# The opening of a two-layer image kernel: first image kept on chip, layer 1's parameters loaded singly, its first rows, queries and values earlier

## The chip, the core and the metric

The kernel runs on one core of a Trainium2 chip. The core has a matrix engine (TensorE, PE in the profile; loading a weight tile into it is listed as PEld), three engines for element-wise work (VectorE or DVE, ScalarE or ACT, GpSimd or POOL) and a sync engine (SP), which here does nothing but issue transfers. Each engine takes its instructions in order and waits at an instruction until its inputs are there and its output buffer is free. Tiles lie in an on-chip memory of 128 partitions, SBUF; matmuls write to a smaller one, PSUM; arrays that fit in neither lie in device memory and are moved by DMA. SP and ACT each have a DMA queue of their own. The metric is the device time of one execution in microseconds (us), as the median of several.

## What is computed

Everything is float32. The input is eight images of 256 channels and 64 x 64 pixels. Two residual layers follow one another, each behind a normalisation over groups of 8 channels of a whole image.

```python
x = x + _L0_conv_ref(_gn(x), ...)
x = x + _L1_conv_ref(_gn(x), ...)

# layer 0
x1 = _conv1x1(x, w1, b1)                  # 32 channels
x2 = _conv1x1(x, w2, b2)                  # 32 channels
x3 = _conv1x1(x, w3, b3)                  # 256 channels
h = relu(_bn(concatenate([x1, _unfold3(reflect_pad(x2))])))
h = relu(_bn(_conv1x1(h, cw1)))           # 32 channels
w = _conv1x1(h, cw2, cb2).reshape(B, G, K * K, H, W)     # 32 groups, 9 taps
x3u = _unfold3(zero_pad(x3)).reshape(B, G, SHARE, K * K, H, W)
out = einsum('bgskhw,bgkhw->bgshw', x3u, w)

# layer 1
q, k, v = three 1x1 convolutions, 256 to 256 channels, 4 heads
att = softmax(q . (unfold7(k) + unfold7(position)))      # 49 neighbours
out_att = sum over the neighbours of att * unfold7(v)
wts = softmax over 9 of einsum('oc,bchw->bohw', Wfc, x)  # 9 weights per channel
oc = nine depthwise pairs: _dwconv(relu(_dwconv(x, w1)), w2)
out_conv = sum over 9 of oc * wts
return rate1 * out_att + rate2 * out_conv
```

So a band of pixels of layer 0 needs the rows of x3 above and below it, and layer 1 of an image needs the statistics of all of layer 0's output for that image.

## The kernel before

**Tiling.** Each image is cut into NB = 8 bands of R = 8 rows (512 pixels); the 256 channels are NCT = 2 tiles of 128. A tile of one band and all channels is 512 KB. All 64 bands of layer 1 are done one after the other by a main loop over g; layer 0 runs AHEAD = 12 bands in front, so the loop starts at g = -12, and for g below 0 only layer 0 is at work ("alone" in the code).

**Order.** The order of the instructions on each engine is the order of the code (`manual_schedule`, L963). Each g has STEPS = 8 steps s, and each step calls `advance()` six times. `after(n, f)` (L215) puts f behind n further advances; that is how work is staggered by hand. For each step `steer(g, s)` (L941) issues loads and statistics, and `beside(g, s)` (L869) gives two lists of work: `mid` runs in the middle of the step, `end` at its end.

**One band of layer 0**, spread over several g:

- `load_x` (L97) brings 512 KB of x into a tile. `first_stats` (L275) calls it for the statistics of layer 0's normalisation and puts the statistics (L283, on DVE) n advances later. For the first image the eight bands go, in this order, into two tiles "xc", two "xr", one "xs" and three "yp" (L965 on). Only the two in "xc" are kept for the convolutions; `steer` loads the bands from 2 on a second time into "xc" at s = 0 of each g below 0 (L99 in the queue's timeline).
- At g, for band g + 12: `small_maps` (L320) computes x1 and x2 on PE, `write_maps` copies them out (L343 and L347 on ACT, edge copies on POOL), `value_maps` (L362) computes x3 (L369), copies it on ACT into x3n (L374) and stores it to device memory from SP.
- For band g + 11: `hidden_maps` (L409) does the first two steps towards the tap weights. `x_by_group` (L399) loads the residual x into "xg", and `values_by_group` (L381) reads x3 back with its neighbouring rows as "x3q" (L389 to L397). Both are laid out with the 32 groups times four pieces of a band on the partitions.
- For band g + 10: `tap_weights` (L441), once for each of three rows of taps. PE makes the weights of three taps (pw, L447); DVE makes the product of weights and x3q for each tap (L460), two product buffers "prod" in turn; POOL adds the product to xg (L468, six to nine of them a band). While layer 0 is alone, every third product goes instead into a "yp" tile and is summed by PE with an identity matrix (`gather`, L481), and DVE adds that sum to xg (`combine`, L488). Then come the statistics of layer 1's normalisation (L496) and the store of the new x as "x1" (L500, four DMAs from SP).

**Layer 1's parameters** are wq, wk, wv (256 KB each), wfc (eight of the nine weights, 2 MB), a mask for the scores, c2 (layer 0's last weights) and last, the ninth of Wfc. `load` at first only keeps their transfers in the list `late`. `layer1_loads` (L186) issues all of them on ACT's queue in one go, after the statistics of the first image. Three operations on them follow later on DVE: wv is scaled by rate1 (L195), and `last` is subtracted from each half of wfc (L200, 128 x 2048 elements):

```python
        for n, f in enumerate(layer1_loads()):
            after(4 * STEPS * (3 + n), f)
```

**Layer 1 begins** at g = 0. Before it, at g = -1, `beside` asks for the first image's first rows: `load_rows` (L528) reads band 0 into "yp" at s = 0 and band 1 at s = 1, from x1; `normalise` (L540, L543 on ACT) follows one and two steps later, a channel tile each. `values` (L551, PE L563, copies on ACT L572, L581) and `value_tile` (L601, PE L607, copy L609 into one of nine "vt" buffers) prepare the values; `position` (L616) makes the positional term on POOL; `queries` (L627, PE L637, ACT L641) and `keys` (L646, PE L658, DVE L666 and L673) prepare the first channel tile. Where the position, queries and keys go is set by these lines:

```python
        early = inx in (0, NB - 1)
        if 0 <= g + 1 < B * NB:
            if s == 5 - early:
                mid.append(lambda: position(bn, inx))
            if s == 6 - early:
                mid.append(lambda: queries(bn, inx, 0))
            if s == 7 - early:
                mid.append(lambda: keys(bn, inx, 0))
```

At g = -1 that is s = 4, 5 and 6; values come at s = 4 and 5, value tiles at s = 6 and 7, and the tap weights of band 9 at s = 0, 2 and 4. From g = 0 on, each step does one head pair of scores (`scores`, PE L703; DVE L712, which adds the mask and finds the maximum, is its first reader), `exponentials` (L720), `probabilities` (DVE L727, ACT L729), the transposition (L735) and the weighted sum (L747) of earlier steps, two of the eight `branch_weights` (PE L825, ACT L830) of a channel tile with the sums of them on POOL (L1026), and a share of the depthwise convolutions (DVE L782, L808).

Of the kernel before, what the change touches and what calls it, by code (L numbers as in the profile page):

```python
# [18 lines left out]
P = 128  # L19
C = 256  # L20
# [40 lines left out]
AHEAD = NB + 4  # L61
AHEAD0 = AHEAD + NB + 1
STEPS = NCT * NT // 2


TAPS_AT = (1, 3, 5), (0, 2, 4)
# [20 lines left out]
def conv_layers_kernel(ctx: ExitStack, tc: tile.TileContext, ins: dict, out: bass.AP):  # L87
# [5 lines left out]
    def x_tile(use, b, i):  # L93
        bufs = {"xs": 1, "xc": 2, "xr": 2}[use]
        return w0.tile([P, NCT, BAND], F32, tag=use, name=f"{use}_{b}_{i}", bufs=bufs)

    def load_x(b, i, use, t=None):  # L97
        t = x_tile(use, b, i) if t is None else t
        nc.sync.dma_start(  # L99
            out=t, in_=x_in[b].rearrange("(t p) n -> p t n", p=P)[:, :, i * BAND : (i + 1) * BAND]  # L100
        )
        return t


    late = []
# [1 line left out]
    def load(name, shape, src=None, now=True):  # L107
        t = const.tile(shape, F32, name=f"c_{name}")
        late.append(lambda: nc.scalar.dma_start(out=t, in_=ins[name] if src is None else src))
        if now:  # L110
            late.pop()()
        return t
# [12 lines left out]
    wk = load("wk", [P, NCT, C], ins["wk"].rearrange("(t p) n -> p t n", p=P), now=False)  # L125
    wv = load("wv", [P, NCT, C], ins["wv"].rearrange("(t p) n -> p t n", p=P), now=False)
    wfc_in = ins["wfc"].rearrange("(t p) k n -> p t k n", p=P)
    wfc = load("wfc", [P, NCT, KK - 1, C], wfc_in[:, :, : KK - 1], now=False)

    ident = const.tile([P, P], F32, name="ident")  # L130
    make_identity(nc, ident)
# [53 lines left out]

    def layer1_loads():  # L186


        last = w1.tile([P, NCT, 1, C], F32, tag="rec", name="last", bufs=1)
        for f in late:  # L190
            f()
        nc.scalar.dma_start(out=last, in_=wfc_in[:, :, KK - 1 :])

        def first():
            nc.vector.tensor_scalar(wv, wv, rate1, None, ALU.mult)  # L195

        def difference(kt):
            nc.vector.tensor_sub(wfc[:, kt], wfc[:, kt], last[:, kt].to_broadcast([P, KK - 1, C]))  # L200

        return [first, lambda: difference(0), lambda: difference(1)]

    class Image:
        def __init__(self):
# [66 lines left out]
        after(3, a1)  # L272


    def first_stats(b, i, use="xs", t=None, n=9):  # L275
        im = images[b]
        if i == 0:
            im.st0 = stat.tile([P, NCT, NB, 6], F32, tag="st", name=f"st0_{b}")
        x = load_x(b, i, use, t)

        def take():
            for ct in range(NCT):
                nc.vector.bn_stats(im.st0[:, ct, i, :], x[:, ct, :])  # L283

        after(n, take)
        return x
# [33 lines left out]
    def small_maps(b, i):  # L320


        im = images[b]

        p12 = ps.tile([P, R // 2, W], F32, tag="gen", name=f"p12_{b}_{i}", bufs=5)
        for kt in range(NCT):
            for u in range(2):
                nc.tensor.matmul(
                    p12[64 * u : 64 * u + 64], im.w12s[:, kt, :],
                    im.xc[i][:, kt, u * BAND // 2 : (u + 1) * BAND // 2],  # L330
                    start=(kt == 0), stop=(kt == NCT - 1),
                )
        return lambda: write_maps(b, i, p12)
# [28 lines left out]
    def value_maps(b, i, mt):  # L362

        im = images[b]
        if mt == 0:
            im.x3[i] = dram.tile([C, R, HP], F32, tag="x3", name=f"x3_{b}_{i}")
        p3 = ps.tile([P, BAND], F32, tag="gen", name=f"p3_{b}_{i}_{mt}", bufs=5)
        for kt in range(NCT):
            nc.tensor.matmul(  # L369
                p3, im.w3s[:, kt, mt * P : (mt + 1) * P], im.xc[i][:, kt, :],  # L370
                start=(kt == 0), stop=(kt == NCT - 1),
            )
        p3 = p3.rearrange("p (r c) -> p r c", r=R)
        nc.scalar.activation(x3n[mt][:, :, 1 : 1 + W], p3, AF.Identity, bias=im.bias[:, 1 + mt : 2 + mt])  # L374
        nc.sync.dma_start(out=im.x3[i][mt * P : (mt + 1) * P], in_=x3n[mt])
# [225 lines left out]
    def value_tile(b, j, u):  # L601
        im = images[b]
        n = min(R, WP - j * R) * KW
        pvt = ps.tile([CHUNK, 2, C], F32, tag="gen", name=f"pvt_{b}_{j}_{u}", bufs=5)
        for g in range(2):
            for ct in range(NCT):
                nc.tensor.transpose(pvt[:n, g, ct * P : (ct + 1) * P], im.vc[j, ct][:, 2 * u + g, :n], ident)  # L607
        vt = im.vt[j, u] = w1.tile([CHUNK, 2, C], F32, tag="vt", name=f"vt_{b}_{j}_{u}", bufs=9)
        nc.scalar.copy(vt[:n], pvt[:n])  # L609

    def new_keys(i):
# [257 lines left out]
    def beside(g, s):  # L869

        b, i = divmod(g, NB)
        bn, inx = divmod(g + 1, NB)
        mid, end = [], []

        early = i in (0, NB - 1)
        if g >= 0:
            if s == 2 - early:
                mid.append(lambda: queries(b, i, 1))
            if s == 3 - early:
                mid.append(lambda: keys(b, i, 1))  # L880
        early = inx in (0, NB - 1)
        if 0 <= g + 1 < B * NB:
            if s == 5 - early:
                mid.append(lambda: position(bn, inx))
            if s == 6 - early:
                mid.append(lambda: queries(bn, inx, 0))
            if s == 7 - early:
                mid.append(lambda: keys(bn, inx, 0))

        if g >= 0 and i < NB - 1:  # L890
            if s in (4, 5):
                mid.append(lambda: values(b, i + 2, s - 4))
            if s in (6, 7):
                end.append(lambda: value_tile(b, i + 2, s - 6))
        if g > 0 and i and s in (0, 1):
            mid.append(lambda: value_tile(b, i + 1, s + 2))
        if i == NB - 1 and 0 <= b + 1 < B:
            if s in (4, 5):
                mid.append(lambda: values(b + 1, 0, s - 4))
            if s in (6, 7):  # L900
                end.append(lambda: value_tile(b + 1, 0, 2 * s - 12))
                end.append(lambda: value_tile(b + 1, 0, 2 * s - 11))
        if g >= 0 and i == 0:
            if s == 0:
                mid += [lambda: values(b, 1, 0), lambda: values(b, 1, 1)]
                end.append(lambda: value_tile(b, 1, 0))
            if s in (1, 2):
                mid.append(lambda: value_tile(b, 1, 2 * s - 1))
            if s == 1:
                end.append(lambda: value_tile(b, 1, 2))  # L910

        nxt = [(b, i + 2, 0)] if g >= 0 and i + 2 < NB else []
        if i == NB - 1 and 0 <= b + 1 < B:
            nxt = [(b + 1, 0, 0), (b + 1, 1, 1)]
        for bb, ii, d in nxt:
            if s == d:
                end.append(lambda bb=bb, ii=ii: load_rows(bb, ii))
            if s in (d + 1, d + 2):
                end.append(lambda bb=bb, ii=ii, d=d: normalise(bb, ii, s - d - 1))

        alone = g < 0
        if 0 <= g + AHEAD < B * NB:
            bq_, iq = divmod(g + AHEAD, NB)
            if alone and s == 0:
                mid.append(lambda: small_maps(bq_, iq)())
            if s == (2 if alone else 0):
                (mid if alone else end).append(lambda: value_maps(bq_, iq, 0))
            if s == (3 if alone else 1):
                mid.append(lambda: value_maps(bq_, iq, 1))
        if 0 <= g + AHEAD - 1 < B * NB and s == (2 if alone else 1):  # L930
            at = (3, 7, 8, 12, 16) if alone else (5, 13, 14, 19, 21)
            end.append(lambda: hidden_maps(*divmod(g + AHEAD - 1, NB), at))
        if 0 <= g + AHEAD - 2 < B * NB and s in TAPS_AT[alone]:
            u = TAPS_AT[alone].index(s)
            end.append(
                lambda: tap_weights(*divmod(g + AHEAD - 2, NB), u, g < -1, PRODUCTS_AT[g < -1][u])
            )
        return mid, end

    def steer(g, s):  # L940

        b, i = divmod(g, NB)
        if s == (2 if g >= 0 else 3) and i == NB - 2 and 0 <= b + 1 < B:
            norm_rows(b + 1)
        n = g + AHEAD + 1
        if s == 2 and n % NB == 0 and 0 < n < B * NB:
            scaled_weights(n // NB)
# [14 lines left out]

    with tc.manual_schedule():  # L963

        for i, use in enumerate(("xc", "xc", "xr", "xr", "xs", None, None, None)):  # L965
            t = None
            if use is None:
                t = w1.tile([P, NCT, RP, W], F32, tag="yp", name=f"x_{i}", bufs=3)
                t = t.rearrange("p t r c -> p t (r c)")[:, :, :BAND]
            x = first_stats(0, i, use, t)  # L970
            if use == "xc":
                images[0].xc[i] = x
            advance()
        for r in range(NB, AHEAD0 - AHEAD):
            first_stats(*divmod(r, NB))
# [2 lines left out]
        scaled_weights(0)  # L978
        for _ in range(32):
            advance()  # L980
        for n, f in enumerate(layer1_loads()):
            after(4 * STEPS * (3 + n), f)

        pending, before, conv = [], None, None
        for g in range(-AHEAD, B * NB):
# [144 lines left out]
```

## Time and profile before

| | us |
|---|---|
| median of 3 runs (4151.52 to 4157.1) | 4152.74 |
| the profiled execution | 4152.64 |
| its span, from the first to the last instruction | 4150.9 |
| PE busy in the span | 4022.6 (97%) |
| DVE, ACT, POOL busy | 3591.9, 3081.0, 2923.0 |

The mean granted clock of PE in this execution is 0.993 of full speed. Read by stage, the span has two very different parts:

| stretch, us | what runs | PE busy | DVE | ACT | POOL | DMA share |
|---|---|---|---|---|---|---|
| 0 to 112 | loads, first statistics, layer 0 alone | 72.59 | 68.78 | 43.51 | 51.47 | 0.81 |
| 112 to 216 | layer 0 alone | 79.90 | 85.84 | 40.99 | 75.10 | 0.87 |
| 216 to 248 | layer 1's first rows, queries, keys, values | 25.35 | 22.55 | 17.25 | 27.41 | 0.88 |
| 248 to 4150 | both layers | 3844.77 | 3414.75 | 2979.20 | 2769.05 | 0.32 |

An engine's busy time is the sum of its instructions' durations in the stretch; DMA share is the mean busy share of the core's 16 DMA engines. The first instruction on the scores (L712) starts at 248.24.

### The profile page before, as it was taken

Reading aid. Unit: us, or ns where it says so; the run is one execution under the profiler, and the core shown is the slowest. Engines: PE = TensorE matmul, PEld = TensorE weight load, DVE = VectorE, ACT = ScalarE, POOL = GpSimd, SP = SyncE. Lnnn points to the kernel's source line nnn. Section 1 sums busy time; section 2 is a strip of 40 time slices with the busy share of each in tenths; the row PEclk is TensorE's granted clock in tenths of the full one; section 3 lists DMA queues with packets and bytes.
Section 4 is the critical chain, followed back from the end, with each engine's and each line's share of the span. In section 5 each row is a group of like instructions: output and inputs, shape, how many; then the busy total and the mean of one; then the engine's idle time right before and its main releaser. Section 6 shows DMA issues by size and latency. Waiting matters only on the chain.

```text
span 4150.9 us, 72735 instructions
## 1 busy us (share of the span) xinstructions
PE 4022.6 (97%) x25292; PEld 2126.8 (51%) x25292; DVE 3591.9 (87%) x7248; ACT 3081.0 (74%) x7726; POOL 2923.0 (70%) x1902
## 2 busy tenths in 40 slices
PE   6789999999999999999999999999999999999998
PEld 3345555555555555555555555555555555455554
DVE  5878998899898898889998898888988889977777
ACT  3467778777787777877778777777778777687776
POOL 4767777677786777777777777777777677744554
PEclk8999999999999999999999999999999999999999
DMA  8854234234244233334234234244233233111100
GB/s 226 194 135 111 73 91 109 72 94 109 62 101 107 76 94 98 81 94 109 72 85 118 72 94 105 66 101 106 71 82 99 65 87 85 33 41 39 39 28 21
DMA packets 381264, 367.89 MB, mean 89 GB/s; under 512 B 55648, under 2 KB 282720, under 8 KB 380640
## 3 DMA queue, kind: packets, MB, share of 16 engines
q1 hardware_dynamic: 377568, 358.68, 34.3%
q8 instruction: 200, 3.28, 0.3%
q10 hardware_dynamic: 3328, 4.55, 0.3%
q14 instruction: 168, 1.38, 0.1%
HBM read 261.42 MB, written 101.71 MB: 87 GB/s over the span
## 4 chain that ended last, share of the span: by engine, by line
PE 71%; DVE 14%; POOL 6%; ACT 5%; DMA 2%; issue 2%; SPq 1%; POOLq 0%; ACTq 0%; DVEq 0%
PE pf L825 33%; PE ptp L735 5%; PE sco L747 5%; PE pk L658 5%; PE sco L703 5%; PE p L369 5%; DVE prod L460 4%; PE pq L637 4%; POOL xg L468 3%; PE pvt L607 2%; PE pv L563 2%; DVE acc L808 2%; PE pw L447 2%; DVE acc L782 2%; POOL ex L1026 2%
## 5 line engine op out<-in xcount | busy, mean ns | idle before, releaser
L825 PE MATMUL pf<-yp,c_wfc 128*128 128x512 f32 x4096 | 1930.5, 595 | 10.6 <-ACT vc L581 5.0
L468 POOL TENSOR_TENSOR xg<-xg,prod 128x1024 f32<-128x1024 f32 x549 | 1203.9, 2193 | 96.6 <-DVE prod L460 64.1
L825 PEld LDWEIGHTS pf<-yp,c_wfc 128*128 128x128 f32 x4096 | 729.9, 190 | 690.5 <-issue 619.4
L1026 POOL TENSOR_TENSOR ex<-ex,ex 128x1024 f32<-128x1024 f32 x384 | 907.7, 2364 | 61.9 <-ACT ex L830 57.2
L830 ACT ACTIVATE ex<-pf 128x512 f32<-128x512 f32 x1024 | 607.3, 593 | 297.9 <-POOL ex L1026 141.3
L782 DVE SCALAR_TENSOR_TENSOR acc<-yp,c_chan,acc 128x504 f32<-128x504 f32 (+3 forms) x1104 | 766.2, 694 | 42.3 <-ACT acc L773 21.7
L460 DVE SCALAR_TENSOR_TENSOR prod<-pw,c_par,x3q 128x1040 f32<-128x1040 f32 x576 | 733.9, 1281 | 66.8 <-PE pw L447 21.6
L808 DVE SCALAR_TENSOR_TENSOR acc<-hid,c_chan,acc 128x504 f32<-128x504 f32 (+3 forms) x1024 | 757.8, 740 | 20.2 <-ACT acc L802 2.1
L855 POOL TENSOR_TENSOR ex<-ex,rec 128x512 f32<-128x512 f32 x127 | 162.3, 1278 | 809.5 <-DVE rec L850 767.1
L729 ACT ACTIVATE prob<-prob,tot 128x196 f32<-128x196 f32 x1024 | 411.6, 450 | 387.2 <-DVE tot L727 386.4
L712 DVE CUSTOM_DVE_ANT_0 prob<-sco,c_mask 128x196 f32<-128x196 f32 x1024 | 325.5, 355 | 272.4 <-PE sco L703 272.0
L720 ACT ACTIVATE prob<-prob,nmax 128x196 f32<-128x196 f32 x1024 | 461.4, 454 | 46.9 <-DVE nmax L712 45.3
L747 PEld LDWEIGHTS sco<-pt,vt 112*64 112x64 f32 x8160 | 283.8, 137 | 182.3 <-issue 51.7
L737 ACT COPY pt<-ptp 112x512 f32<-112x512 f32 x511 | 297.0, 581 | 105.0 <-PE ptp L735 103.0
L735 PE MATMUL ptp<-ident,prob 128*112 128x128 f32 x2044 | 341.7, 287 | 31.2 <-ACT prob L729 30.5
L747 PE MATMUL sco<-pt,vt 112*64 112x64 f32 x8160 | 347.0, 227 | 0.0
L735 PEld LDWEIGHTS ptp<-ident,prob 128*112 128x112 f32 x2044 | 203.9, 133 | 201.4 <-issue 77.7
L703 PE MATMUL sco<-kb,qb 64*64 64x196 f32 x4096 | 295.2, 357 | 0.0
L563 PE MATMUL pv<-yp,c_wv 128*128 128x512 f32 (+2 forms) x576 | 247.3, 554 | 0.6
L369 PE MATMUL p<-xc,w3s 128*128 128x512 f32 x512 | 244.4, 601 | 0.0
L658 PE MATMUL pk<-yp,c_wk 128*128 128x512 f32 (+2 forms) x576 | 240.8, 545 | 0.0
L637 PE MATMUL pq<-yp,c_wq 128*128 128x512 f32 x512 | 240.6, 592 | 0.0
(140 smaller groups left out, 5294.0 us busy)
## 6 DMA issues: line engine op xcount, KB each, us to landing
x<-x3n SPq DMA_DIRECT2D x128, 264.0 KB, 2.1
x3q<-x SPq DMA_DIRECT2D x128, 264.0 KB, 7.2
xc<-in_x SPq DMA_DIRECT2D x64, 512.0 KB, 5.0
xg<-in_x SPq DMA_DIRECT2D x256, 128.0 KB, 4.8
x<-xg SPq DMA_DIRECT2D x256, 128.0 KB, 2.4
yp<-x SPq DMA_DIRECT2D x128, 256.0 KB, 3.3
xr<-x SPq DMA_DIRECT2D x64, 512.0 KB, 5.8
out_x<-xr SPq DMA_DIRECT2D x64, 512.0 KB, 3.1
```

The lines of the kernel that those rows point to most:

```text
L369: nc.tensor.matmul(p3, im.w3s[:, kt, mt * P : (mt + 1) * P], im.xc[i][:, kt, :], start=(kt == 0), stop=(kt == NCT - 1),)
L460: nc.vector.scalar_tensor_tensor(prod[:, :, :RUN], pw[:, j, :RUN].unsqueeze(1).to_broadcast([P, SHARE, RUN]), par[:, PCB2 + k : PCB2 + k + 1],
L468: nc.gpsimd.tensor_add(im.xg[i], im.xg[i], rows(prod))
L703: nc.tensor.matmul(sco[half[t], h, :NKEY], qb[half[h], 2 * m + t].rearrange("p r c -> p (r c)"), kb[half[h], :, c0 : c0 + KW], start=True, ...
L720: nc.scalar.activation(prob[:, h, :NKEY], prob[:, h, :NKEY], AF.Exp, bias=nmax[:, h : h + 1], scale=-1.0, accum_out=tot[:, h : h + 1],)
L735: nc.tensor.transpose(ptp[:, h, ch], prob[:, h, ch * CHUNK : (ch + 1) * CHUNK], ident)
L747: nc.tensor.matmul(po[half[h], :, t * TQ : (t + 1) * TQ], im.vt[i + ch, m][:n, t, (2 * ct + h) * HD : (2 * ct + h + 1) * HD], pt[:n, h, ch ...
L782: nc.vector.scalar_tensor_tensor(o, yp[:, ct, ra + dr : rb + dr, ca + dc : cb + dc], chan[:, ct, CW1 + k : CW1 + k + 1], o, ALU.mult, ALU.add,
L808: nc.vector.scalar_tensor_tensor(o, hid[:, ra + dr : rb + dr, ca + dc : cb + dc], chan[:, ct, CW2 + k : CW2 + k + 1], o, ALU.mult, ALU.add,)
L825: nc.tensor.matmul(pf, wfc[:, kt, 2 * m + j, ct * P : (ct + 1) * P], images[b].yp[i][:, kt, PAD : PAD + R], start=(kt == 0), stop=(kt == N ...
L830: nc.scalar.activation(ex[:, j].rearrange("p (r c) -> p r c", r=R), pf, AF.Exp)
L1026: after(4, lambda ex=ex, exb=exb: nc.gpsimd.tensor_add(ex, ex, exb))
```

## The change

The change has three parts, and all of them lie in the opening and the handover to layer 1.

1. All eight bands of the first image are kept from the first load on: bands 0 and 1 in "xc" and 2 and 3 in "xr" as before, bands 4 to 7 as two halves each in the buffers "vt" of layer 1's values, which are free until then. `load_x` now gives a list with one view for each channel tile. Since `images[0].xc` holds all eight, `steer` loads none of the bands 2 to 7 a second time. "xs" and "yp" aren't used for the first image any more.
2. Of layer 1's parameters only c2 is loaded at once. The others follow one by one, half of a g (24 advances) apart, still on ACT's queue: wq at g = -10, s = 0, wk at s = 4, wv at g = -9, s = 0, the mask at s = 4, the two halves of wfc at g = -8, s = 0 and s = 4, and last at g = -7, s = 0. The three operations on them (L195, L200) move from their former places to the ends of the steps 2, 3 and 4 of g = -1.
3. Before layer 1's first band: position(0, 0) is computed at the start; the rows of bands 0 and 1 are loaded at the ends of the steps 5 and 7 of g = -2; both normalisations of band 0 stand at the beginning of g = -1; the first queries come at s = 2 and the keys at s = 3 of g = -1 (before: 5 and 6), the values at 3 and 4 (4 and 5), the value tiles at 5 and 6 (6 and 7). The tap weights of band 9, computed in the same g, move from s = 0, 2, 4 to s = 3, 5, 7.

```diff
+PLACES = 6
...
-    def load_x(b, i, use, t=None):
-        t = x_tile(use, b, i) if t is None else t
-        nc.sync.dma_start(
-            out=t, in_=x_in[b].rearrange("(t p) n -> p t n", p=P)[:, :, i * BAND : (i + 1) * BAND]
-        )
-        return t
+    def load_x(b, i, use):
+
+        x = x_in[b].rearrange("(t p) n -> p t n", p=P)[:, :, i * BAND : (i + 1) * BAND]
+        if use == "vt":
+            halves = []
+            for ct in range(NCT):
+                t = value_store(f"x_{b}_{i}_{ct}").rearrange("p g c -> p (g c)")
+                nc.sync.dma_start(out=t, in_=x[:, ct])
+                halves.append(t)
+            return halves
+        t = x_tile(use, b, i)
+        nc.sync.dma_start(out=t, in_=x)
+        return [t[:, ct] for ct in range(NCT)]
+
+    def value_store(name):
+
+        return w1.tile([P, 2, C], F32, tag="vt", name=name, bufs=9)
...
-    wfc = load("wfc", [P, NCT, KK - 1, C], wfc_in[:, :, : KK - 1], now=False)
+    wfc = const.tile([P, NCT, KK - 1, C], F32, name="c_wfc")
...
         last = w1.tile([P, NCT, 1, C], F32, tag="rec", name="last", bufs=1)
-        for f in late:
-            f()
-        nc.scalar.dma_start(out=last, in_=wfc_in[:, :, KK - 1 :])
+        for kt in range(NCT):
+            late.append(lambda kt=kt: nc.scalar.dma_start(out=wfc[:, kt], in_=wfc_in[:, kt, : KK - 1]))
+        late.append(lambda: nc.scalar.dma_start(out=last, in_=wfc_in[:, :, KK - 1 :]))
...
-        return [first, lambda: difference(0), lambda: difference(1)]
+
+        late.pop(0)()
+        for n, f in enumerate(late):
+            after(PLACES * (4 + n) * STEPS // 2, f)
+        for n, f in enumerate((first, lambda: difference(0), lambda: difference(1))):
+            after(PLACES * (11 * STEPS + 3 + n), f)
...
-        early = inx in (0, NB - 1)
+        early = 4 if g == -1 else inx in (0, NB - 1)
         if 0 <= g + 1 < B * NB:
-            if s == 5 - early:
+            if s == 5 - early and g >= 0:
                 mid.append(lambda: position(bn, inx))
...
         if i == NB - 1 and 0 <= b + 1 < B:
-            if s in (4, 5):
-                mid.append(lambda: values(b + 1, 0, s - 4))
-            if s in (6, 7):
-                end.append(lambda: value_tile(b + 1, 0, 2 * s - 12))
-                end.append(lambda: value_tile(b + 1, 0, 2 * s - 11))
+            lead = 1 if g < 0 else 0
+            if s in (4 - lead, 5 - lead):
+                mid.append(lambda: values(b + 1, 0, s + lead - 4))
+            if s in (6 - lead, 7 - lead):
+                end.append(lambda: value_tile(b + 1, 0, 2 * (s + lead) - 12))
+                end.append(lambda: value_tile(b + 1, 0, 2 * (s + lead) - 11))
...
+        if g == -2 and s in (5, 7):
+            end.append(lambda: load_rows(0, (s - 5) // 2))
         for bb, ii, d in nxt:
-            if s == d:
+            if s == d and g >= 0:
                 end.append(lambda bb=bb, ii=ii: load_rows(bb, ii))
-            if s in (d + 1, d + 2):
+            if s in (d + 1, d + 2) and (bb, ii) != (0, 0):
                 end.append(lambda bb=bb, ii=ii, d=d: normalise(bb, ii, s - d - 1))
...
-        if 0 <= g + AHEAD - 2 < B * NB and s in TAPS_AT[alone]:
-            u = TAPS_AT[alone].index(s)
+        d = 2 if g == -1 else 0
+        if 0 <= g + AHEAD - 2 < B * NB and s - d in TAPS_AT[g < -1]:
+            u = TAPS_AT[g < -1].index(s - d)
...
+        if (g, s) == (-1, 0):
+            for ct in range(NCT):
+                normalise(0, 0, ct)
...
-        for i, use in enumerate(("xc", "xc", "xr", "xr", "xs", None, None, None)):
-            t = None
-            if use is None:
-                t = w1.tile([P, NCT, RP, W], F32, tag="yp", name=f"x_{i}", bufs=3)
-                t = t.rearrange("p t r c -> p t (r c)")[:, :, :BAND]
-            x = first_stats(0, i, use, t)
-            if use == "xc":
-                images[0].xc[i] = x
+        for i in range(NB):
+            images[0].xc[i] = first_stats(0, i, "xc" if i < 2 else "xr" if i < 4 else "vt")
             advance()
...
-        for n, f in enumerate(layer1_loads()):
-            after(4 * STEPS * (3 + n), f)
+        layer1_loads()
+        position(0, 0)
```

More of the change, by code (lines that the diff above doesn't have):

```diff
@@ L272, in gn_affine, with first_stats @@
         after(3, a1)
-    def first_stats(b, i, use="xs", t=None, n=9):
+    def first_stats(b, i, use="xs", n=9):
         im = images[b]
@@ L278, in first_stats @@
             im.st0 = stat.tile([P, NCT, NB, 6], F32, tag="st", name=f"st0_{b}")
-        x = load_x(b, i, use, t)
+        x = load_x(b, i, use)
         def take():
             for ct in range(NCT):
-                nc.vector.bn_stats(im.st0[:, ct, i, :], x[:, ct, :])
+                nc.vector.bn_stats(im.st0[:, ct, i, :], x[ct])
         after(n, take)
@@ L329, in small_maps @@
                     p12[64 * u : 64 * u + 64], im.w12s[:, kt, :],
-                    im.xc[i][:, kt, u * BAND // 2 : (u + 1) * BAND // 2],
+                    im.xc[i][kt][:, u * BAND // 2 : (u + 1) * BAND // 2],
                     start=(kt == 0), stop=(kt == NCT - 1),
@@ L369, in value_maps @@
             nc.tensor.matmul(
-                p3, im.w3s[:, kt, mt * P : (mt + 1) * P], im.xc[i][:, kt, :],
+                p3, im.w3s[:, kt, mt * P : (mt + 1) * P], im.xc[i][kt],
                 start=(kt == 0), stop=(kt == NCT - 1),
@@ L607, in value_tile @@
                 nc.tensor.transpose(pvt[:n, g, ct * P : (ct + 1) * P], im.vc[j, ct][:, 2 * u + g, :n], ident)
-        vt = im.vt[j, u] = w1.tile([CHUNK, 2, C], F32, tag="vt", name=f"vt_{b}_{j}_{u}", bufs=9)
+        vt = im.vt[j, u] = value_store(f"vt_{b}_{j}_{u}")
         nc.scalar.copy(vt[:n], pvt[:n])
```

## The prediction

> **What bounds the kernel now.** I read the page's 40 slices first, then a table of windows by stage, then the chain of waits of the opening, then each queue's timeline there.
>
> ```profile
> PE   6789999999999999999999999999999999999998
> DMA  8854234234244233334234234244233233111100
> ```
>
> ```profile
> 112.00:216.00 104.00, 79.90 (x411) 39.31 (x411) 85.84 (x104) 40.99 (x76) 75.10 (x55) 0.93 0.87 199
> 216.00:248.00 32.00, 25.35 (x123) 13.67 (x122) 22.55 (x32) 17.25 (x41) 27.41 (x17) 0.89 0.88 215
> ...
> 380.00:4150.00 3770.00, 3716.94 (x23675) 1971.24 (x23673) 3307.34 (x6795) 2879.38 (x7282) 2685.28 (x1722) 1.00 0.32 81
> ```
>
> (Columns: window, length, busy us of PE, weight load, DVE, ACT, POOL, granted clock, DMA share, GB/s.) From 248 on, PE is busy 99% of the time; an opening of 248 us stands ahead, in which layer 0 runs alone and no engine is full, while DMA is at 0.87. The diff touches only the opening and the first steps after it: in the built orders the reuse of PSUM and SBUF slots is the same from the end of the first eighth of band 0 on. So an opening that is shorter by some us makes the kernel shorter by as many.
>
> What sets the opening's pace is a loop through memory.
>
> ```profile
> 138.48 1.91 SPq L389 DMA_DIRECT2D x3q<-x  x3
> 140.43 0.61 SPq L397 DMA_DIRECT2D x3q<-x  x1
> 141.13 0.55 SPq L99 DMA_DIRECT2D xc<-in_x  x1
> 147.74 0.34 SPq L375 DMA_DIRECT2D x<-x3n  x1
> 149.59 2.56 SPq L500 DMA_DIRECT2D x<-xg  x4
> ```
>
> ```profile
> 139.78 6.78 DMA x3q<-x
> ...
> 148.48 1.09 DVE xg L488
> 149.59 0.58 SPq L500
> ```
>
> The sum of one band (L488) stands on DVE behind the first product (L460) of the next band, which waits for that band's x3q. Only then can SP store x1 (L500), and behind that store stand xs, x3, xg and the next x3q. One round: product 1.3, statistics 0.6, sum 1.2, SP's issues from 149.6 to 160.7, landing 166.8. The L488 starts on DVE's timeline (71.41, 91.67, 109.60, 129.42, 148.40, 168.08, 186.75, 204.62) are 20.3, 17.9, 19.8, 19.0, 19.7, 18.7 and 17.9 apart. The last round was held by POOL, not by the load (product at 203.40, its wait put down to POOL's add): six adds of 2.2 and the small copies give nearly the same period.
>
> ```profile
> 60.30 2.28 DVE L200 TENSOR_TENSOR c_wfc<-c_wfc,last 128x2048 f32<-128x2048 f32 x1
> ```
>
> ```profile
> 60.36 11.01 POOL L468 TENSOR_TENSOR xg<-xg,prod 128x1024 f32<-128x1024 f32 x4
> ```
>
> Four adds at 2.26 would take 9.0; they took 11.0 beside the subtraction.
>
> [...] by size, the packets of xc (2048 B) start at 144.5, when those of x3q (264 to 1056 B) run out. [...]
>
> **The change part by part,** against the profiled execution, 4152.64 us (span 4150.9, 1.7 around it; 0.1 under the median of 4152.74).
>
> *Six loads of xc go* (bands 2 to 7, 512 KB). In the steady rounds each is issued after x3q and its data move after x3q's, in time that ends in a gap (DMA share 0.04 and 0.00 at 129 to 131). SP's 0.55 lies in a wait for x3n (141.7 to 147.7). So it frees the tail of the queue, which nobody waits for: I take 0.3 for each of the last two rounds that lose it, -0.5; not a loss; at most the rounds of bands 1 to 3 sink to 17.9, -5.4.
>
> *The start.* Between 26 and 66 DMA is full: 3.2 MB of layer 1's parameters and 1.5 MB of xc are in it, both gone now. xg is issued at 42.42 to 45.1 and x3q to 49.5 with or without them (they follow ACT's x3n), x3q(0) lands at 54.1. With an empty queue: xg 2.6, then x3q's 1.08 MB at the 200 GB/s seen for such packets, 5.4, and about 1 to land: 51.8, so -2.3. From there POOL's six adds are the chain, up to the sum at 71.4; the first subtraction (L200) is no longer among them: -2.0. Together -4.3. The second L200 (75.07) lay where x3q was waited for anyway: 0. Reading bands 4 to 7 as eight halves costs four more issues of about 0.6 on SP beside a full DMA, 0; position(0, 0), 1.37 on POOL, goes to where POOL idles 28 us: 0.
>
> *Parameters, one at a time on ACT's queue.* Each issue is 0.48 on ACT (from 24.7 to 27.7 in the timeline), ACT is 39% busy: 0. [...] The 2 MB of wfc moved at about 400 GB/s (8192 B packets, 29 to 34), so half takes 2.6. Half 0 is issued where band 2's x3q is on its way: +2.6 on the loop (bounds 0 and 2.6). Half 1 comes right after x3n of band 4, partly in the gap: +1.5 (0 to 2.6). "last" falls into band 3's x3q: +0.7. The three 256 KB loads and the mask fall where POOL's adds are the chain: 0 (at most 2.4). Besides, [...] (SP's yp issue at 219.69 waited on x3q): ACT then waits for an xg of SP's before it may issue half 0, up to 4 us, ahead of the maps (L343); those are wanted only some us later, 0, else up to +4. Sum +4.8.
>
> The opening up to 216 is thus -0.5 - 4.3 + 4.8 = 0.0.
>
> *Handover (216 to 262).*
>
> ```profile
> 224.58 0.97 ACT L543 ACTIVATE yp<-yp,aff 128x704 f32<-128x704 f32 x1 [2.09 <-DMA yp<-x]
> ```
>
> ```profile
> 241.05 1.30 DVE L460 SCALAR_TENSOR_TENSOR prod<-pw,c_par,x3q 128x1040 f32<-128x1040 f32 x1 [2.15 <-POOL xg L468]
> 242.27 0.74 DVE L666 SCALAR_TENSOR_TENSOR kb<-pk,c_chan,pe 128x512 f32<-128x512 f32 x1
> ...
> 248.24 0.35 DVE L712 CUSTOM_DVE_ANT_0 prob<-sco,c_mask 128x196 f32<-128x196 f32 x1
> ```
>
> Before, the keys stand behind nine products that POOL's adds pace, and are made at 242.3. After, by the built order: the rows of band 0 no longer stand behind xc (1.6 less): 222.9. Both normalisations now stand ahead of the eight map copies on ACT: 224.8, maps +3.8 to 228.6. PE: queries 1.7, p3 1.7, keys 2.4: 230.6. DVE: keys at 230.6 to 232.3, twelve us sooner. But then L200 2.3 (234.6), two products (237.0), L200 again (239.3); the first add starts at 235.8 and is blocked by that to 240.2; with two product buffers the others follow adds of 2.26, the sixth product ends at 248.2; five taps 1.6, a seventh product 1.3: the first L712 at 251.1, 2.9 later. ACT's list (two vc of 1.84, x3n, hidden maps 2.3, vt) puts the first score matmul at 245.5, 0.8 sooner, but L712 waits for DVE. Part of the 2.9 is regained, since the table load (1.28) and two vt copies no longer stand behind L712; product and two taps ahead of the reciprocal (L727) cost 1.9 again. Second L712: +1.3, and PE is full from there. Bounds: -4 (adds not blocked, DVE keeps up with PE) to +6 (pv and pf wait for PSUM slots that the late products hold).
>
> Sum: 0.0 + 1.3: 4153.9.
>
> **Rivals.** *Faster, 4141:* the queue's traffic is what keeps rounds above 17.9. For: DMA 0.87, far above any engine's need. Against: x3q stands ahead of xc, and POOL's adds floor the round. Price: -5.4 for three rounds, -4.3 at the start, parameters in the gaps 0, handover -2: -11.7. *Slower, 4166:* the parameters' turns and ACT's waits for SP's landings. Place: the rounds of bands 1 to 3. Price: 5.2 for wfc, 2.8 for four small ones, 4 for ACT's wait, -4.3 at the start, handover +6 instead of 1.3: +13.7. It decides once x3n comes later than the sum, which in the round at 147.7 has 1.9 of slack. *The change does nothing:* out, the built SP order lacks the six loads.
>
> **Chances.** A measurement tells about 0.2%, 8.3 us, from no change. Forecast 0.42, own range 4147 to 4160; faster rival 0.37 (4132 to 4147: down to there if the rounds of bands 4 to 6 sink to 17.9 too, -3.7, and the handover gives 4 more); slower rival 0.21 (4159 to 4172). Some of each rival is within 8.3: faster 0.33, same 0.48, slower 0.19. Range 4136 to 4166: it holds both rivals' figures and leaves under a tenth out on each side.
>
> **What would show it.** Right: L488 of band 0 near 67; rounds of bands 1 and 2 longer by 2 each, x3q landing with 8192 B packets among its own; later rounds as before; one add of 4.3 near 236; first L712 at 250 to 252, L666 at 230. Wrong: rounds of 17.9 without xc; scores before 245; or rounds over 22 with ACT idle at its DMA issues.

## The result, and the profile after

The changed kernel takes 4169.8 us (median of 7 runs, 4167.92 to 4172.44) against 4152.74: 1.0041 times as long, 95% interval 1.0029 to 1.0052. It is 17 us slower; 4153.9 was forecast, and the range ended at 4166. The profiled execution took 4169.96 (span 4168.2, clock 0.989). In the changed kernel, lines near `load_x` lie some 10 further down than before, and those behind `layer1_loads` 16: the sum `combine` is L504, the loads of x3q are L405 to L413, the first reader of the scores is L728.

The page's slices of PE and DMA, after:

```profile
PE   5889999999999999999999999999999999999998
DMA  6863343343343333343334333244233233111100
```

The windows by stage (columns as before; each stage as long as it now is):

```profile
112.00:225.00 113.00, 89.77 (x447) 44.30 (x447) 92.09 (x112) 46.74 (x86) 82.01 (x62) 0.94 0.82 187
225.00:263.00 38.00, 28.11 (x132) 14.80 (x130) 25.21 (x33) 19.40 (x46) 21.61 (x13) 0.91 0.85 204
394.00:4150.00 3756.00, 3714.80 (x23627) 1969.89 (x23625) 3295.98 (x6777) 2873.00 (x7270) 2677.77 (x1719) 1.00 0.32 81
```

The main part is what it was: PE is busy 99% of it. The opening is longer, and PE is already less busy in the first slice. The chain of waits of the opening names the place (start, length, what):

```profile
77.43 10.33 DMA c_wfc<-in_wfc
...
89.01 9.10 DMA x3q<-x
...
99.51 1.22 DVE xg L504
...
109.47 5.51 DMA last<-in_wfc
...
115.58 4.15 DMA x3q<-x
121.26 1.23 DVE xg L504
```

From the sum of band 0 (69.71) to that of band 1 (99.51) 29.8 us pass, before 20.3; to the next 21.75, before 17.93. Most of that stretch on the chain is now transfers of layer 1's parameters and x3q behind them; the first half of wfc, priced at 2.6, lands 10.3 after its issue. SP's timeline and SP's waits show what the prediction hadn't thought of:

```profile
79.74 0.62 SPq L405 DMA_DIRECT2D x3q<-x  x1
80.44 0.60 SPq L409 DMA_DIRECT2D x3q<-x  x1
87.78 1.84 SPq L405 DMA_DIRECT2D x3q<-x  x3
```

```profile
SPq L405 <- DMA c_wfc<-in_wfc: 6.7, 1, 6.7
SPq L405 <- DMA last<-in_wfc: 5.3, 1, 5.3
```

SP stops in the middle of a band's x3q for 6.7 us until the half of wfc, a transfer of the other queue, has landed: the half lands at 87.76, and SP goes on at 87.78. A round later it stops for 5.3 behind `last`. SP's other stops for a parameter in this trace are 1.4 for wq, 6.0 for wk, 4.8 for wv and 1.0 for the mask. In the built program's order of transfers, both queues counted together, each of these six stops stands at the eighth transfer behind the one that it waits for.

The sum of what moved, by the profiled spans: first sum 1.7 earlier, rounds 1 and 2 longer by 9.5 and 3.8, rounds 3 to 7 shorter by 1.7 together: the eighth sum is 9.9 later (214.56 for 204.62). From there to the first scores 48.2 pass instead of 43.6, +4.6, which makes 14.5. Band 0 is then 0.6 shorter, and 3.4 come in the main part (the last section). Together 17.3.

### The profile page after: what moved, and what is told of

It reads as the page before. It is cut to its first block, busy times and chain, and to the rows that moved or that the text cites. A ratio compares the mean times of both kernels' runs of the same rounds, so it can differ in the third digit from the quotient of the medians.

```text
span 4168.2 us, 72729 instructions
## 1 busy us (share of the span) xinstructions
PE 4027.5 (97%) x25292; PEld 2129.8 (51%) x25292; DVE 3590.9 (86%) x7248; ACT 3079.7 (74%) x7726; POOL 2922.9 (70%) x1902
## 4 chain that ended last, share of the span: by engine, by line
PE 71%; DVE 14%; POOL 6%; ACT 4%; DMA 2%; issue 2%; SPq 0%; POOLq 0%; ACTq 0%; DVEq 0%
PE pf L841 33%; PE ptp L751 5%; PE sco L763 5%; PE p L385 5%; PE pk L674 5%; PE sco L719 5%; DVE prod L476 4%; PE pq L653 4%; POOL xg L484 3%; PE pvt L623 2%; PE pv L579 2%; DVE acc L824 2%; PE pw L463 2%; DVE acc L798 2%; POOL ex L1045 2%
## 5 line engine op out<-in xcount | busy, mean ns | idle before, releaser
L728 DVE CUSTOM_DVE_ANT_0 prob<-sco,c_mask 128x196 f32<-128x196 f32 x1024 | 325.4, 355 | 271.9 <-PE sco L719 271.4
L862 DVE RECIPROCAL rec<-ex 128x256 f32<-128x256 f32 x128 | 224.4, 1753 | 4.4
```

## The experiments

The profiled readings of all runs, in us. "Rounds" are the distances of the first three sums, "scores" is from the eighth sum to the first scores. Ratios are to runs of the kernel before on the same chip, where its median was 4154.1 to 4156.6, some us above 4152.74; so an expected time is best compared by its distance to the kernel before. A caution for single readings: the first sum comes between 68.4 and 72.5 in runs whose code up to there differs in a subtraction or the position at most, so differences of 2 us at the start say little.

| kernel | ratio (95% interval) | first sum | round 1 | round 2 | eighth sum | scores |
|---|---|---|---|---|---|---|
| before | | 71.41 | 20.26 | 17.93 | 204.62 | 43.62 |
| changed | 1.0041 (1.0029 to 1.0052) | 69.71 | 29.80 | 21.75 | 214.56 | 48.18 |
| e1_last_later | 1.0032 (1.0019 to 1.0044) | 69.68 | 28.73 | 18.43 | 211.82 | 47.96 |
| e2_burst | 1.0005 (0.9996 to 1.0013) | 68.40 | 19.51 | 18.24 | 201.81 | 48.75 |
| e3_resident | 0.9996 (0.9988 to 1.0004) | 69.78 | 19.39 | 18.28 | 201.66 | 43.95 |
| e4_single | 1.0038 (1.0026 to 1.0051) | 73.92 | 24.25 | 21.51 | 217.83 | 46.84 |
| e5_wfc_no_wait | 1.0026 (1.0015 to 1.0037) | 72.16 | 27.60 | 18.76 | 214.06 | 47.98 |
| e6_wfc_behind_x3q | 1.0013 (1.0006 to 1.0020) | 70.95 | 21.67 | 19.26 | 208.44 | 48.28 |
| e7_handover_early_sub | 0.9999 (0.9991 to 1.0007) | 72.48 | 18.67 | 18.25 | 202.86 | 47.99 |
| e8_late_sub_only | 1.0009 (1.0001 to 1.0017) | 71.71 | 20.10 | 18.71 | 204.76 | 51.65 |
| e9_half_a_g_later | 1.0018 (1.0011 to 1.0025) | 70.48 | 20.67 | 18.44 | 208.25 | 48.60 |
| e10_halves_apart | 1.0023 (1.0015 to 1.0031) | 70.87 | 27.48 | 18.63 | 215.92 | 47.81 |
| e11_store_later | 0.9966 (0.9954 to 0.9979) | 71.12 | 18.53 | 16.39 | 192.59 | 42.24 |
| e12_taps_back | 1.0009 (1.0000 to 1.0017) | 71.24 | 19.07 | 18.64 | 203.19 | 48.96 |
| e13_norm_behind_maps | 0.9996 (0.9987 to 1.0004) | 70.00 | 18.68 | 18.39 | 199.79 | 47.13 |

### Which part of the change costs: e2, e3, e4

Parameters in a burst again, on the changed kernel:

```diff
-        for n, f in enumerate(late):
-            after(PLACES * (4 + n) * STEPS // 2, f)
+        for f in late:
+            f()
```

> The changed kernel with all of layer 1's parameters issued at once on ACT's queue as before the change; the rest of the change stays. If the parameters' single loads carry the loss: the rounds between the first three sums (29.8 and 21.75) fall to the 20.3 and 17.9 of before, the first sum comes about 2 later again (71.5 for 69.7), the time is 4158 to 4159. If the handover or the resident image carries it: the rounds fall, but the time stays at 4165 or more.

Only part 1 of the change, and only part 2, each on the kernel before:

> The kernel before with the first image kept on chip alone (no reload of bands 2 to 7; parameters in a burst, handover as before). Prediction's step: nobody waits for the tail of the queue, so the rounds keep their 17.9 to 20.3, and the time changes by -0.5 to -3 (some of it at the start): 4150 to 4152. Queue-traffic rival: the rounds of bands 1 to 6 sink to about 17.9 each, 4144 to 4147.

> The kernel before with layer 1's parameters loaded one by one alone, at the places of the change; the scaling of wv and the two subtractions from wfc follow in g = -6, which the later landing needs; bands 2 to 7 are still loaded twice, handover as before. Single-loads theory (waits or traffic): rounds 1 and 2 grow as in the changed kernel, by 9 to 13 together, the start gains 0 to 2, the time is 4161 to 4166. If instead the loss needs the other parts, it is 4150 to 4155.

The single loads carry most of it. Taken out of the change they leave 1.0005, with both rounds at their old length; put alone into the kernel before (with the subtractions in g = -6) they cost 1.0038, nearly the whole loss. But in e4 rounds 1 and 2 grow by 7.6 together and not by the expected 9 to 13; the first scores come 16.4 later than before, and the other 8.8 are spread over the first sum (2.5), rounds 3 to 7 (3.1) and the handover (3.2), which no run explains. The first image on chip alone changes the time by less than can be told (0.9996), as the step of the prediction said; its rounds stay between 17.6 and 20.5 and don't sink to 17.9. What is left in e2_burst is the handover: 48.75 to the first scores.

### Waits or turns: e1, e5, e10, e9, e6

Two things in the single loads could hold x3q: SP's wait for a landing, and the bytes that move beside x3q ("turns" below). These runs only move the last three loads, by steps of the main loop counted from its start. In e5:

```diff
-            after(PLACES * (4 + n) * STEPS // 2, f)
+            after(PLACES * (16, 20, 24, 28, 34, 36, 44)[n], f)
```

The last three numbers are half 0, half 1 and `last`. In the changed kernel they are 32, 36, 40; in e1 32, 36, 44; in e10 34, 42, 44; in e9 36, 44, 52; in e6 30, 38, 46, with `nc.sync` in place of `nc.scalar` for these three.

> The changed kernel, with one edit: last (256 KB, the ninth weights) is issued half a g later on ACT's queue, so that the eighth transfer behind it is a store of x1 and no longer one of the loads of band 3's x3q; the bytes and the round in which they move stay about the same. Wait theory (SP's x3q load waits for the landing of the eighth transfer before it): the wait of 5.3 us on SP in the round from sum 1 to sum 2 goes, that round falls from 21.75 to about 18.7, the time from 4169.8 to about 4167. Traffic theory (the parameter's bytes take turns with x3q): the round stays at 21 to 22, the time at 4170.

> The changed kernel with the first half of wfc issued two steps later on ACT's queue (behind the maps of band 4), and last half a g later. The half still moves in the round between the first two sums, while band 2's x3q is on its way, and the second half follows it as before; but the eighth transfers behind the two halves are now stores that come after x3q, so that no load of x3q waits for a landing of wfc. Wait theory: the first round falls from 29.8 to 21 to 23 (2.6 of traffic left on top of 20.3), the first x3q loads of it are issued without a pause on SP, the time is about 4159 to 4161. Traffic theory: the round stays at 27 or more, the time at 4166 or more.

In e1 the second round falls to 18.43, and SP's wait for `last`, now 1.7, stands at a store of x1. In that run `last` also moved behind the landing of x3q, so its bytes left the round with the wait. But in the changed kernel only 6 of its 256 packets have started by 112 us, when most of the x3q issued up to then has (272, 313 and 138 packets a us from 110 on), and SP's stop is 5.3: most of the 3.3 that the round lost is the wait.

In e5 SP issues the loads of x3q without a stop for wfc, and the chain still has

```profile
86.69 11.67 DMA x3q<-x
...
98.54 0.06 DVE prod L476
...
99.76 1.23 DVE xg L504
```

Round 1 is 27.6. So the wait theory's number fails, and a half of wfc that moves beside x3q costs nearly as much as the stop did. That doesn't make the stop cheap in the changed kernel, for e5 puts the one in place of the other: in the changed kernel the packets of half 0 move from 80.0 to 86.9, while SP stands still before most of x3q's loads. The load of x3q on the chain tells the two apart, in the kernel before and in e4_single:

```profile
82.74 7.59 DMA x3q<-x
```

```profile
SPq L394 <- DMA c_wfc<-in_wfc: 6.8, 1, 6.8
```

```profile
90.94 5.89 DMA x3q<-x
```

| kernel | that load issued, us after the first sum | on its way | round 1 |
|---|---|---|---|
| before | 11.3 | 7.6 | 20.3 |
| e4_single | 17.0 | 5.9 | 24.3 |
| changed | 19.3 | 9.1 | 29.8 |
| e5_wfc_no_wait | 14.5 | 11.7 | 27.6 |

e4 has the same stop, but issues half 1 only at 92.19, when x3q is nearly done; its round is 4.0 longer than before. The changed kernel's is 5.5 longer again. The load is issued 2.3 later (1.0 of it is another wait of SP, for the landing of the mask) and is on its way for 3.2 more, beside half 1, issued at 87.98: x3q's packets of 1056 B start at 135, 76, 23 and 22 a us from 89 on, while up to 45 of half 1 do; in e4, ahead of half 1, at 182, 245 and 85. So by these single readings the 9.5 of round 1 are about 4 of stop behind half 0, 2.3 of later issue and 3.2 of turns with half 1.

As to the turns, I then expected each half to cost its own duration.

> As e5_wfc_no_wait, with the second half of wfc six steps later, so that it meets the x3q of band 3 and not that of band 2. Large-packet theory: each half holds up the x3q that it meets by its own duration at over 300 GB/s, 3 to 4 us: round 1 falls from 27.6 to 23 to 24, round 2 grows from 18.8 to 21 to 23, the sum of the two stays within 2. If the first half alone does the harm (by its place ahead of the small rows of x3q): round 1 stays at 26 or more and round 2 at 19.

Neither number of the first theory came: round 1 stays at 27.5 and round 2 at 18.6. In e5 and e10 the first half alone does the harm, and the second, once most of x3q has moved, none. The packets that started in each us of e10's round 1 show how, beside e2's, where x3q is alone:

```text
e10, us              84   85   86   87   88   89   90   91   92   93   94   95   96
x3q, 264 to 1056 B  317  203   57   43   42   27  137  176  238  167    5   15   31
wfc, 8192 B           0    7   18   23   32   34    9    1    1    2    1    0    0
e2, us               79   80   81   82   83   84   85   86
x3q, 264 to 1056 B  220  325  203  222  253  278   28    7
```

In the four us in which both queues start packets steadily (86 to 89), x3q starts 27 to 57 a us, about one to three for each of wfc's, instead of over 200: in this trace a packet of 8 KB takes 0.42 us here, one of 1056 B 0.09 (medians). The prediction reckoned with the sum of the bytes alone. What divides the DMA engines between the two queues isn't shown.

Of the 8.0 between e10 and e2 part lies ahead of the turns (SP issues the last load of x3q 15.9 after the sum, in e2 12.4; 1.4 is a wait for the mask's landing), and part is a tail: a few packets of wfc move until 95.4, the last of x3q start after 96, and x3q has landed at 97.0, when its last packet has. What delays these few is not shown.

> The changed kernel with the two halves of wfc and last still on ACT's queue, but each issued later: first half half a g later, second half and last one g and one and a half g later, which puts each of them behind the maps of a band, about when that round's x3q has landed. Large-packet theory (once 8 KB packets of wfc are in turn with x3q's packets of about 1 KB, x3q hardly moves until they are done): no x3q is on its way any more, rounds 1 to 3 are 19 to 21, the eighth sum comes at 204 to 207, the time is 4157 to 4161. If parameters cost by their bytes alone, wherever they come on this queue: the rounds' sum stays some 10 above that of e2_burst, 4166 or more.

> The changed kernel with the two halves of wfc and last issued by SP instead of ACT, each right behind the x3q of one of the bands 2, 3 and 4, where the second loads of x stood before the change: same bytes in the same rounds, but behind x3q in its own queue. Wait and traffic theory both: the rounds fall to 18 to 20.5, the eighth sum comes at 203 to 206, and what is left over before is the handover: first scores near 252, 4157 to 4160. If layer 1's parameters cost by their bytes wherever they stand in the opening: rounds over 21, 4165 or more.

Both took the halves out of x3q's way and won most of it back: e9 has 20.67 in round 1, e6 21.67, and the ratios fall to 1.0018 and 1.0013. By their distance to the kernel before on the same chip (7.0 and 6.0 us) both times lie where they were expected, but the eighth sums come 1.3 and 2.4 later than expected. In e9 no x3q is on its way when the second half moves, yet round 3 takes 23.21; SP shows why:

```profile
110.83 6.84 SPq L516 DMA_DIRECT2D x<-xg  x4
117.72 0.60 SPq L109 DMA_DIRECT2D xs<-in_x  x1
118.42 0.43 SPq L391 DMA_DIRECT2D x<-x3n  x1
118.90 2.69 SPq L421 DMA_DIRECT2D xg<-in_x  x4
```

The four stores of x1, 2.6 us elsewhere, take 6.84 (SP's waits put 4.4 on a landing of wfc), and the next x3q stands behind them. That is the wait alone, without turns: the round is 3.5 longer than e2's (19.71).

### The handover: e7, e8, e12, e13

e7 is e2_burst with the two subtractions back at their early places; e8 is e3_resident with only the subtractions late (`after(6 * (11 * STEPS + 3 + n), f)`).

> Resident first image, parameters in a burst, the two subtractions from wfc where they stood before the change, and the earlier rows, queries, keys and values with the later tap weights of the changed kernel. Against e2_burst (4156.6; eighth sum to first scores 48.75) only the subtractions are moved out of g = -1. Subtraction theory (2 x 2.3 on DVE ahead of the first products, one of POOL's adds blocked by the second): first scores 5 to 7 earlier after the eighth sum (42 to 44), 4150 to 4152. Order theory (the later tap weights themselves hold the first scores): 46 to 48.75 remain, 4154 to 4157.

> Resident first image, parameters in a burst and handover as before; only the scaling of wv and the two subtractions from wfc are moved to the end of steps 2 to 4 of g = -1, as in the changed kernel. Subtraction theory: the eighth sum comes 1 to 1.5 earlier than in e3_resident (201.7), the first scores 4 to 6 later after it (43.95 there), 4154 to 4157. Order theory: within 2 of e3_resident (4152.4).

In the changed kernel the long add that the prediction named is there, 4.13 for 2.26, and the subtraction that runs beside it is longer too, 3.29 for 2.28:

```profile
250.16 4.13 POOL xg L484
```

```profile
248.94 3.29 DVE L211 TENSOR_TENSOR c_wfc<-c_wfc,last 128x2048 f32<-128x2048 f32 x1
```

But in the changed order the subtractions cost 0.8 at the first scores (48.75 to 47.99), while the same move costs 7.7 in the old order (43.95 to 51.65). They aren't the 4.6. Another wait is at the head of two queues of the changed kernel:

```profile
234.03 1.85 ACT L559 ACTIVATE yp<-yp,aff 128x704 f32<-128x704 f32 x2 [10.54 <-DMA yp<-x]
235.79 1.39 ACT L359 ACTIVATE x<-p,bias 32x252 f32<-32x252 f32 x3
```

```profile
235.06 3.78 PE L653 MATMUL pq<-yp,c_wq 128*128 128x512 f32 x4 [5.78 <-ACT yp L559]
```

ACT waits 10.5 us for band 0's rows with the map copies behind it, PE 5.8 with everything behind it. To separate this from the later tap weights, e12 undoes these alone in e7 (`s in TAPS_AT[alone]` again), and e13 then swaps two groups on ACT:

```diff
-        if (g, s) == (-1, 0):
-            for ct in range(NCT):
-                normalise(0, 0, ct)
+        if (g, s) == (-1, 1):
+            end += [lambda: normalise(0, 0, 0), lambda: normalise(0, 0, 1)]
```

> e7_handover_early_sub with one part of the handover undone: the tap weights of band 9 go back to steps 0, 2 and 4 of g = -1; rows, normalisation, queries, keys and values stay as in the changed kernel. Order theory (the later tap weights put the first product behind queries, keys and values on PE, and POOL's adds of 2.26 each then pace DVE up to the first scores): first product after the eighth sum at 24 to 28 instead of 33.7, first scores 41 to 44 after it instead of 48, 4149 to 4152. Rows theory (layer 1's first rows land too late, and all stands behind the normalisation on ACT): the first product is early, but keys and scores stay where they are, first scores 46 to 48 after the eighth sum, 4153 to 4156.

> e12_taps_back with one edit: the two normalisations of band 0 stand behind the eight map copies of band 11 on ACT instead of ahead of them. Queue-head theory (the normalisation waits for its rows at the head of ACT's queue, and the maps, POOL's edge copies and adds and with them the last sum alone wait behind it): the maps run about 4 to 6 earlier, the ninth sum comes 20 to 24 after the eighth instead of 28.3, the first scores 43 to 46 after it instead of 49, the time is 4151 to 4155. If layer 1's first rows themselves set the first scores (through queries, keys and values on PE): they stay at 47 or more, 4156 to 4160.

e12 contradicts the order theory: 48.96, and a ninth sum 28.3 after the eighth. In e13 the same copies run while the rows are on their way:

```profile
212.19 1.41 ACT L354 ACTIVATE x<-p,bias 32x252 f32<-32x252 f32 x3 [3.46 <-PE p L339]
...
219.36 1.84 ACT L554 ACTIVATE yp<-yp,aff 128x704 f32<-128x704 f32 x2 [3.34 <-DMA yp<-x]
```

The ninth sum comes at 23.4 (28.3), and the time is 3.0 below that of the kernel before on its chip, where e12's is 4.5 above (the two intervals overlap slightly). The first scores come at 47.1, 1.8 sooner, not in the expected 43 to 46 but where the rival had them. So in this order the wait at the head of ACT's queue is shown for the ninth sum and, less firmly, for the time; for the first scores it is a part. In the changed kernel itself, whose ninth sum comes 16.8 after the eighth, the swap wasn't tried. Another 3 us at the first scores between e13 and e3_resident, whose ratios are the same, stay open: in e13 the values' copies stand on ACT ahead of what the last three tap weights need, but that was not tried by itself.

### A version faster than both: e11

The prediction's loop (sum, store, x3q, product, sum) says that the opening is paced by SP's order, not by bytes. One edit on e3_resident puts the store behind the next x3q:

```diff
+            if alone and b == 0:
+                after(18, store)
+            else:
+                store()
```

> e3_resident with one more edit: while layer 0 is alone on the first image, the store of x1 is issued 18 advances later, behind x3q of the next band but one on SP instead of ahead of it. Loop theory of the prediction (sum, store, x3q, product, sum through SP's order): the loop gets a second round of slack, and the rounds fall from 18 to 20.5 to what POOL's adds and the DMA traffic leave, 15.5 to 18; the eighth sum comes at 180 to 198 for 201.7, the time is 4132 to 4149. If DMA traffic sets the rounds, not the loop: they stay at 18 to 20, the time at 4151 to 4153.

0.9966 (0.9954 to 0.9979): 4142.8 us. The windows of the seven rounds, e11 and then e3_resident:

```profile
71.00:192.00 121.00, 100.73 (x511) 49.91 (x510) 109.31 (x117) 54.35 (x100) 96.88 (x73) 0.96 0.77 202
```

```profile
70.00:201.00 131.00, 106.36 (x520) 53.14 (x519) 108.53 (x117) 55.87 (x102) 97.69 (x73) 0.92 0.82 186
```

The same work of DVE and POOL fits into 121 us instead of 131 or so; rounds of 16.4 to 17.0 are now common, and the DMA share has fallen. Removing bytes (e3) hadn't moved them.

## Why the prediction was wrong

*What bounds the kernel* was right: the change acts in the opening alone, and rounds follow the loop through memory (e11).

*Six loads of xc*, -0.5, "the tail of the queue, which nobody waits for": right as far as can be told. e3_resident gives 0.9996, whose interval holds both -0.5 and none.

*The start*, -4.3: the first sum came 1.7 sooner, which by the caution above says little. The x3q of band 0 landed at 53.2, 0.9 sooner and not 2.3, and the time from there to the sum fell by 0.8 and not by 2.0. That the burst was in the way isn't shown: with it this x3q landed at 52.8 in e2 and at 55.1 in e7. SP waited in this stretch for the landing of wq (1.4, within that x3q) and, behind it, of wk (6.0).

*Parameters*, +4.8: this step failed; the first two rounds gave 13.3. Half 0 was priced at 2.6, its bytes at 400 GB/s beside band 2's x3q, and "bounds 0 and 2.6" took that for the worst. It landed 10.3 after its issue, and until then SP could not issue most of that x3q: a stop of 6.7, worth about 4 of the round (e4). A wait of one queue for the other's landing was in the text, but only in one direction: ACT waiting for SP's loads, "up to 4". It is SP that waited for ACT's large transfers, in the middle of the loads on which the loop hangs. Half 1, priced at 1.5 for a gap, fell among x3q's packets and cost about 3; `last`, 0.7, cost 3.3 (e1), most of it the wait. Nor were bytes the price of the turns: where half 0 does move beside x3q, the round is 8.0 longer than with the burst (e10 against e2), and 6.8 longer than in e9, which up to there differs in half 0's place alone.

*Handover*, +1.3: measured +4.6 at the first scores and +3.3 at the second. From keys to first scores it went as worked out, 20.4 against 20.5. Ahead of the keys it didn't. The rows, "1.6 less", landed 19.5 after the eighth sum, 0.5 less than before, as they still stand behind x3q; and the queries took 3.78 instead of 1.7, on a PE that had idled 5.8 and whose granted clock the trace has at one half from 232.0 to 238.9. That ACT's maps stand behind the rows was seen, and priced at their own 3.8; the wait ahead of them was not.

*The slower rival* named the right place, the rounds of bands 1 to 3, and came near with 4166, in part by luck: it had the wait in the wrong direction, and counted 4.3 won at the start and 6 lost in the handover, where 1.7 and 4.6 came.

## What to carry to other kernels

Ask of each transfer that is added which later issue, on either queue, will wait for its landing, and when it will land. In the changed kernel all six stops of SP for a parameter stood at the eighth transfer behind it; 1 MB landed 10.3 us after its issue, not 2.6, and a stop of 4.4 to 6.8 us on SP cost a round 3.3 to 4.0. Price a transfer that moves beside another by the packets that a trace counts, not by bytes alone: in e10 small ones on one queue started at 27 to 57 a us beside packets of 8 KB on the other, instead of over 200, and it was the small ones' landing that the loop waited for. And an operation that is issued "sooner" at the head of an in-order queue is no sooner if its input isn't; what it stops is everything behind it: here ACT waited 10.5 us for band 0's rows, with the map copies behind.

## What else the runs showed of the hardware

The 3.4 us lost in the main part aren't more work. The trace records the granted clock of PE at one half for spells of 3.4 us. Between 330 us and the last 20 us of the program the kernel before has one such spell (at 3537.6), the changed one has spells at 2996.8, 3553.2 and, 6.8 long, at 3611.2. Both programs have the same short pauses of PE at these places, 0.9 us near 2982 (2996 after) and 2.7 near 3594 (3609 after), and the distance between the kernels, read at the first readers of the scores, jumps by 1.7 and 1.9 there; the experiments have between one (e7) and, counted by length, four (e8, e9, e11). So half clock was recorded at pauses of 0.9 and 2.7 us in the changed kernel's execution, and at the same pauses not in that of the kernel before; what decides between the two isn't shown. As an estimate from these traces, a spell of 3.4 us at half clock costs up to 1.7, so two executions with one and with four spells can differ by up to 5 us for this alone.
